# Sixteen heads: the first block's maxima between the steps of the last chunk's chain, projections beside the mixture, one stage elsewhere in memory

## The chip, the cores and the metric

The kernel runs on one core of a Trainium2 chip, in one launch. The metric is the device time of one execution in microseconds (us); the median of three runs is compared. A core has a matrix engine, TensorE (PE; its weight loads are listed apart, as PEld), three engines for everything else, VectorE (DVE), ScalarE (ACT) and GpSimd (POOL), and SyncE (SP), which here issues nearly all transfers (DMAs). Each engine works through its own list of instructions in the order that was fixed when the program was built, and waits where an instruction needs a result of another engine. Data lie in an on-chip memory of 128 partitions (SBUF); matrix products land in eight accumulation banks (PSUM), from which the other engines read them.

## The reference, cut to what matters

A residual stream `x` of 2048 tokens and 128 channels, in float32, goes through twelve steps. Each normalises `x`, computes something and adds it back, the feed-forward parts by half:

```python
x = x + 0.5 * L0_ffn(ln(x)); x = x + L0_attn(ln(x)); x = x + 0.5 * L0_ffn(ln(x))
x = x + 0.5 * L1_ffn(ln(x)); x = x + L1_attn(ln(x)); x = x + 0.5 * L1_ffn(ln(x))
x = x + 0.5 * L2_ffn(ln(x)); x = x + L2_attn(ln(x)); x = x + 0.5 * L2_ffn(ln(x))
x = x + 0.5 * L3_ffn(ln(x)); x = x + L3_attn(ln(x)); x = x + 0.5 * L3_ffn(ln(x))
```

Three of these functions matter here:

```python
def L1_attn(x):                       # 16 heads of 8 channels, every token sees every token
    q, k, v = heads(x @ w_qkv.T)
    attn = softmax((q * 8 ** -0.5) @ k.T)
    return merge(attn @ v) @ w_proj.T + b_proj
def L2_attn(x):                       # the same, q and k rotated by position, no bias
    q, k, v = heads(x @ Wqkv)
    q, k = q * cos + rotate_half(q) * sin, k * cos + rotate_half(k) * sin
    ...
def L1_ffn(x):                        # "the mixture": a shared expert and eight gated ones
    w = the two largest gates of softmax(ln'(x) @ gate_w.T), made to sum to one
    return swiglu_shared(x) + sum(w[:, e] * swiglu_e(x) for e in range(8))
def L2_ffn(x):                        # "the quantised stage"
    scale = max over blocks of 32 of |x| / 7.5; round x / scale to the FP6 grid; same for W
    return dequantised(x) @ dequantised(W).T + bias
```

## The kernel before, in words

**Tiles.** The 2048 tokens are four chunks (`NC` = 4) of `CH` = 512, a chunk is `TC` = 4 tiles of `P` = 128. `xs[c]` holds chunk c of the stream on chip through all twelve stages; nothing of it goes to memory between them. The stages in order are ffn0, attn0, ffn0, ffn1 (the first mixture), attn1 (the first attention of sixteen heads), ffn1 (the second mixture), ffn2 (the quantised stage), attn2 (the second attention of sixteen heads), ffn2, ffn3, attn3, ffn3; k counts a function's first and second use.

**Stages as generators.** Each stage is a Python generator that issues instructions and gives control back at its `yield`s. Class `Stage` (L2066 to 2111) holds one. `prepare` opens the stage's early memory pool on one of two sides of the memory, left or right in turn (`sides[n % 2]`), lets `pre_...` fetch weights, and makes the generator. While a stage runs it can call `io.lead(passed)`: this lowers the next stage's `due` by the time said to have passed, and when that is at or under 0 advances the next stage by one step. `mark(c)` tells that chunk c of a stage is done, `ready(c)` asks that of the stage before, `here()` asks whether the stage is the running one; `upcoming()` prepares the next stage. `yield True` says that what can be led is done; then the main loop (L2121 to 2128) runs the generator to its end when its turn comes. So the last chunk's work of each stage, which needs the previous stage's last chunk, stands at the seam of two stages. A scheduler settles each engine's list from the order of issue, with two exceptions: instructions kept in program order (`pe(...)`), and a context of high priority, whose instructions are put ahead.

**The mixture** (ffn1, L664 to 760). For each chunk nine experts follow each other. `up` makes twelve products of 512 columns, a SiLU on ACT and the product `h` on DVE (L717); `down` makes the products `pd` (L725, sixteen matmuls in the trace) and adds each tile into `xs[c]`, weighted by the gate, on DVE (L735). In the second mixture, with the quantised stage's steps between, 26 of these `h` start from 1574.6 to 1698.0 us, one every 4.9. After each expert of chunks 2 and 3 stands `if c > 1: io.lead(4.3)` (L756).

**The quantised stage** (ffn2, L807 to 838, with `quantised`, L763 to 794). Per chunk: statistics, `rs` (power on POOL, L143), `xn`, ten DVE operations of quantising (scales, `y`, `e2`, `big`) with one on POOL, four transposes, a copy `qT` on ACT, four products, an addition into `xs[c]`. In its first use chunks 0 to 2 are led beside the second mixture and the fourth stands behind it; its tiles have two buffers there.

**The sixteen-head attentions** (`packed`, L1296 to 1622, which attn0 with eight heads also uses). Per chunk, `front` transposes the normalised chunk and splits it into a high and a low part (`xH`, `xL`); `queries_or_keys(n, c)` multiplies by weights split in the same way (three products of 512 columns for `product`; attn2 makes two such products, multiplies each by a table and adds them on POOL: `rotated`, L1680, six products) and splits the result again (`kH`, `kL`, `qH`, `qL`). `stack_k` and `stack_q` copy rows of these by DMA (`rows_of`, three DMAs each, on SP's queue) into tiles `km` and `qt`, where a head's eight channels stand beside their low parts and constant rows; POOL fills the tiles by memsets first (L1493 to 1496). Before, the part that can be led (L1343 to 1354) makes the fronts and keys of chunks 0 to 2 and the queries of chunk 0, but the tiles, memsets and copies come behind `yield True`, so when the stage runs.

**Two passes of softmax** (`flash`, L970 to 1264). The work is cut into blocks n = (head group of 4 heads, query chunk): 16 blocks for each attention. `stream_a` is the first pass: for each block 32 steps, each with two score products (L1069, 512 columns each, into a pair of banks `s1`, of which there are two) and a maximum over 2 x 512 scores on DVE (L1087, at high priority). A step's keys come from one chunk; in block 0 the order is chunk pairs outside, query tiles, then the two chunks of the pair. When the 32 are through, DVE forms `mx` (L1095), and `put_max` folds it into the queries (`q2`). `stream_b` is the second pass: scores again (L1190), now with the maximum subtracted in the product, exp on ACT (L1199), products with the values (`pv`, L1136). It is a block or so behind the first pass, so within an attention both run side by side; at its start only the first pass can run. `hook` puts work at points of the first pass: the last chunk's front and keys (`ensure(NC - 1)`) at block 0's start, values, and the next queries (`queue`). Edges that the program adds (`last_of`, `last_top`) hold the first maximum of a group of steps behind a given DVE instruction.

Of the kernel before, what the change touches and what calls it, by code (L numbers as in the profile page):

```python
# [9 lines left out]
F32 = mybir.dt.float32  # L10
# [54 lines left out]
def tile_macaron(ctx: ExitStack, tc: tile.TileContext, a: dict, out: bass.AP, stages=STAGES):  # L65
# [598 lines left out]
    def ffn1(io, k, w, early):  # L664
# [35 lines left out]
        with tc.tile_pool(name="f1", bufs=1) as pool, tc.tile_pool(name="f1w", bufs=1) as pool_w:  # L700
# [42 lines left out]
            for c in range(NC):  # L743
                xT, gate = cur
                for n, e in enumerate(order):
# [10 lines left out]
                    if c > 1:  # L756
                        io.lead(4.3)
# [5 lines left out]
    def quantised(src, pool, tag, bufs=1):  # L763
# [5 lines left out]
        def new(name, m=n):  # L769
            return pool.tile([P, m], F32, name=name, tag=tag + name, bufs=bufs)  # L770
# [25 lines left out]
    def pre_ffn2(k, pool):  # L796
        if k == 0:
            w = fetch(pool, "l2w", 0, C)
            wqT.append(const.tile([P, P], F32, name="wqT"))
            q = quantised(w, pool, "w")  # L800
# [6 lines left out]
    def ffn2(io, k, w, early):  # L807
        bufs = 2 if k == 0 else 1
        half_bias = early.tile([P, C], F32, name="half_bias")
        nc.vector.tensor_scalar_mul(half_bias, row("bias2"), 0.5)  # L810
        for c in range(NC):
            while not io.ready(c):
                yield 0
            if c == NC - 1:
                yield True
                io.upcoming()
                io.lead(9.0)
            xn = layer_norm(c, True)
            q = quantised(xn.rearrange("p i c -> p (i c)"), early, "x", bufs)
            if io.here():  # L820
                for _ in range(8):
# [3 lines left out]
            qT = early.tile([P, CH], F32, name="qT", tag="qT", bufs=bufs)  # L825
# [9 lines left out]
            io.mark(c)  # L835
            if c < NC - 1:
                yield 1.0
                stats_of[c] = statistics_of(xs[c])

# [130 lines left out]
    def flash(io, pool, early, its, nh, causal, scale, s1, s2, pv_mm, put_max, begin, finish, poll=None,  # L970
              on_exp=None, split_at=1, fill=None, leads=None, hook=None, flush=True, order=None):
# [30 lines left out]
        if halved:  # L1002

            halves = {}
            for name in ("ident", "maskq", "maskk"):
                raw = pool.tile([P, 2, P], F32, name="halfraw", tag="halfraw", bufs=2)
# [5 lines left out]
                halves[name] = pool.tile([P, 2, P], BF16, name="half" + name)  # L1012
# [11 lines left out]
        if tiled and causal:  # L1024
            junk = pool.tile([P, CH], F32, name="junk")
            strip = pool.tile([P, CH], F32, name="strip")
# [4 lines left out]
        last_top = {}  # L1031
# [16 lines left out]

        def stream_a():
            for n, (g, qc) in enumerate(its):  # L1050
                begin(n)
                nk = chunks(qc)
                npair = (nk + 1) // 2
                mp = pool.tile([P, TC, nh, NC], F32, name="mp", tag="mp", bufs=3)
                for pi in range(npair):
                    for r in range(TC):
                        before = hook(n, pi, r) if hook is not None else None
                        if pi == r == 0 and before is None:
                            before = last_top.get(n - 1)
                        for kc in range(2 * pi, min(2 * pi + 2, nk)):  # L1060
                            for j0 in range(0, nh, 2):
                                ps = first_pass_bank()
# [1231 lines left out]
```

## Time and profile before

| What | us |
|---|---|
| Median of three runs (3746.23, 3755.47, 3755.72) | 3755.47 |
| The profiled execution, whole | 3769.46 |
| Its span, first to last instruction | 3767.7 |
| PE busy, 25325 matmuls | 3420.8 (91%) |
| DVE busy, 4793 instructions | 2870.9 (76%) |
| ACT busy, 3838 instructions | 2036.2 (54%) |
| POOL busy, 830 instructions | 828.8 (22%) |
| Mean granted clock of PE, as a share of full speed | 0.943 |

The stretches around the change, from windows of the trace (busy time of each engine, granted clock of PE):

| Stretch | From, to | Length | PE | DVE | ACT | POOL | Clock |
|---|---|---|---|---|---|---|---|
| First mixture's end to attn1's first `mx` | 817.5, 874.0 | 56.5 | 30.7 | 44.9 | 5.8 | 7.5 | 0.54 |
| attn1 from there, most of it | 874.0, 1340.0 | 466.1 | 449.7 | 443.7 | 399.7 | 0.0 | 0.99 |
| Second mixture, chunks 1 to 3 | 1580.0, 1702.7 | 122.7 | 120.5 | 88.9 | 37.4 | 13.6 | 1.00 |
| Second mixture's end to attn2's first `mx` | 1702.7, 1780.6 | 77.9 | 47.1 | 66.1 | 12.6 | 18.5 | 0.59 |
| attn2 from there, most of it | 1780.6, 2300.0 | 519.4 | 499.6 | 494.8 | 443.1 | 2.6 | 0.99 |

The table is read by rows: an engine whose busy time is close to the length sets that stretch's pace. Times of single instructions count from the start of the profiled execution's span. The second mixture's row begins at a round number somewhat after that stage's start and shows the engines' loads there.

### The profile page before, as it was taken

How to read it: one execution, taken by the hardware profiler on the slowest of the kernel's cores; microseconds unless marked ns; L12 is line 12 of the kernel's file. 1: busy time of each engine (PE TensorE's matmuls, PEld its weight loads, DVE VectorE, ACT ScalarE, POOL GpSimd, SP SyncE). 2: the span in 40 equal slices, each digit the busy share in tenths (PEclk: the TensorE clock that was granted, in tenths of full speed). 3: DMA queues.
4: the chain of work that ended last, by engine and by line, in shares of the span. 5: the costliest groups of instructions: out<-in, count | busy, mean ns of one | idle time of the engine just before them, and what ended most of it. 6: DMA issues, size and time to landing. Idle time of an engine off the chain costs nothing. (4 is left out here: it accounts for less than half of the span.)

```text
span 3767.7 us, 64628 instructions
## 1 busy us (share of the span) xinstructions
PE 3420.8 (91%) x25325; PEld 1846.5 (49%) x25325; DVE 2870.9 (76%) x4793; ACT 2036.2 (54%) x3838; POOL 828.8 (22%) x830
## 2 busy tenths in 40 slices
PE   7679987978999999996999999888999999999989
PEld 5543356863333333783333333366444444444458
DVE  6488555768999998668899999654777877788862
ACT  3246732325888888421788888732333444444442
POOL 1511124110000000112000000142555445533341
PEclk9779988987999999996999999998899999999999
DMA  3311023000000000102000000012443232221010
GB/s 104 83 49 29 9 81 95 4 26 5 12 12 14 8 3 1 35 1 70 10 14 6 16 5 4 15 46 75 140 147 112 97 106 97 89 63 52 24 34 12
DMA packets 124689, 170.18 MB, mean 45 GB/s; under 512 B 25120, under 2 KB 52514, under 8 KB 124384
## 3 DMA queue, kind: packets, MB, share of 16 engines
q1 hardware_dynamic: 121824, 160.80, 13.7%
q0 software_dynamic: 2560, 5.25, 0.9%
q8 instruction: 199, 3.26, 0.3%
q14 instruction: 106, 0.87, 0.1%
HBM read 101.25 MB, written 45.87 MB: 39 GB/s over the span
## 5 line engine op out<-in xcount | busy, mean ns | idle before, releaser
L1087 DVE TENSOR_REDUCE mp<-s 128x2 f32<-128x1024 f32 (+3 forms) x1440 | 1625.7, 1181 | 88.5 <-PE s L1069 68.1
L1199 ACT ACTIVATE pt<-s 128x512 f32<-128x512 f32 (+1 forms) x2368 | 1220.7, 601 | 216.4 <-PE s L1190 141.8
L1190 PE MATMUL s<-q,km 32*128 32x512 f32 (+2 forms) x2368 | 733.6, 491 | 28.6 <-ACT pt L1199 18.7
L1136 PE MATMUL pv<-pt,v 128*32 128x256 f32 (+1 forms) x8568 | 730.9, 413 | 22.9 <-ACT ov L1577 11.2
L1069 PE MATMUL s<-km,qt 32*128 32x512 f32 (+3 forms) x2368 | 620.0, 507 | 61.1 <-DVE mp L1087 37.1
L1190 PEld LDWEIGHTS s<-q,km 32*128 32x128 f32 (+1 forms) x2368 | 324.1, 184 | 531.6 <-issue 341.3
L1179 ACT ACTIVATE pt<-s 128x512 f32<-128x512 f32 (+3 forms) x640 | 306.2, 530 | 355.7 <-PE s L1171 212.8
L143 POOL TENSOR_TENSOR rs<-rs,minus_half 128x4 f32<-128x4 f32 x56 | 57.5, 1026 | 1543.7 <-DVE rs L142 1542.7
L1993 DVE TENSOR_TENSOR sum<-sum,pt 128x512 f32<-128x512 f32 (+3 forms) x328 | 259.4, 805 | 89.9 <-ACT pt L1179 88.3
L1136 PEld LDWEIGHTS pv<-pt,v 128*32 128x32 f32 x8568 | 169.1, 108 | 316.4 <-issue 146.3
L1171 PE MATMUL s<-q,k 64*128 64x512 f32 (+3 forms) x1920 | 300.0, 403 | 14.7 <-ACT pt L1179 10.4
L1136 PE MATMUL pv<-pt,latv 128*64 128x512 f32 (+3 forms) x1280 | 310.4, 564 | 1.3 <-ACT pt L1179 1.3
L1993 POOL TENSOR_TENSOR sum<-sum,pt 128x512 f32<-128x512 f32 (+1 forms) x200 | 265.6, 1328 | 181.5 <-ACT pt L1179 177.0
L1069 PEld LDWEIGHTS s<-km,qt 32*128 32x128 f32 (+1 forms) x2368 | 236.4, 191 | 124.1 <-DVE mp L1087 82.3
L1171 PEld LDWEIGHTS s<-q,k 64*128 64x128 f32 x1920 | 161.8, 188 | 224.8 <-issue 137.3
L715 ACT ACTIVATE sg<-pg 128x1024 f32<-128x1024 f32 x72 | 73.9, 1027 | 174.4 <-PE pg L229 158.8
L1069 PE MATMUL s<-k,q 64*128 64x512 f32 (+3 forms) x640 | 133.7, 433 | 19.0 <-DVE mp L1087 18.6
L1791 DVE TENSOR_TENSOR rot<-rot,tab 128x512 f32<-128x512 f32 x128 | 87.7, 685 | 74.2 <-PE rot L229 38.4
L725 PEld LDWEIGHTS pd<-l1d,h 128*128 128x128 f32 x1152 | 139.3, 192 | 5.6
L725 PE MATMUL pd<-l1d,h 128*128 128x128 f32 x1152 | 140.1, 275 | 0.0
L717 DVE TENSOR_TENSOR h<-pu,sg 128x1024 f32<-128x1024 f32 x72 | 87.9, 1220 | 60.6 <-PE pu L229 55.7
L1171 PE MATMUL s<-q,two 64*128 64x512 f32 (+3 forms) x640 | 128.0, 368 | 0.0
(575 smaller groups left out, 4696.7 us busy)
## 6 DMA issues: line engine op xcount, KB each, us to landing
tab<-in_l3rope SPq DMA_DIRECT2D x66, 256.0 KB
q<-q SPq DMA_DIRECT2D x32, 512.0 KB
k<-k SPq DMA_DIRECT2D x32, 512.0 KB
l0e<-in_l0e SPq DMA_DIRECT2D x32, 256.0 KB
q<-h SPq DMA_DIRECT2D x32, 256.0 KB
q<-rot SPq DMA_DIRECT2D x32, 256.0 KB
k<-h SPq DMA_DIRECT2D x32, 256.0 KB
k<-rot SPq DMA_DIRECT2D x32, 256.0 KB
```

The costliest lines, as they stand in the source:

```text
L715: nc.scalar.activation(sg, pg, AF.Silu)
L717: nc.vector.tensor_tensor(h.rearrange("p m n -> p (m n)"), pu, sg, ALU.mult)
L725: nc.tensor.matmul(pd[:, i, :], h[:, m, i * P : (i + 1) * P], wd[:, m, :], start=m == 0, stop=m == 1,)
L1069: pe(nc.tensor.matmul(ps[:, o : o + w], lhsT, rhs[:, :w], start=True, stop=not masked))
L1087: ins = nc.vector.tensor_reduce(mp[:, r, j0 : j0 + 2, kc], both[:, :, :w], AX.X, ALU.max,)
L1136: i = pe(nc.tensor.matmul(pv[out_rows, lo:hi], lhsT, pts[j][:, lo:hi], start=kt == 0, stop=kt == nt - 1 and hi == CH))
L1171: pe(nc.tensor.matmul(outs[j][:, c0:], lhsT, rhs[:, c0:], start=i == 0, stop=i == len(terms[0]) - 1 and not diag,))
L1179: ex = nc.scalar.activation(pts[j][:, c0:], outs[j][:, c0:], AF.Exp, scale=scale)
L1190: pe(nc.tensor.matmul(ps[:, c0:], lhsT, rhs[:, c0:], start=i == 0, stop=i == len(terms) - 1 and (tiled or not diag),))
L1199: ex = nc.scalar.activation(pt[:, c0:], ps[:, c0:], AF.Exp, scale=scale)
L1791: nc.vector.tensor_tensor(t.bitcast(F32), ps, halves["tabs"][i], ALU.mult)
L1993: eng.tensor_tensor(t[:, c0:], other[:, c0:], pts[j][:, c0:], ALU.add)
```

## The change

Both programs compute the same thing with the same instructions on PE, DVE, ACT and POOL; SP issues two DMAs more. What changes is where they are issued.

1. `flash` becomes a generator with a number of steps `ahead`. With it, block 0's steps go chunk by chunk of the keys (all four query tiles on chunk 0's keys, then on chunk 1's, and so on), and the first 24 of its 32 steps, which need the keys of chunks 0 to 2 alone, are given out one at a time, each behind a `yield`, and without high priority.
2. In `packed` the helpers move ahead of the part that is led. That part now also fills and stacks the keys of chunks 0 to 2 and the queries of chunk 0, makes chunk 1's queries, and then gives out the 24 steps with an infinite `due` until the last chunk's `ensure(NC - 1)`, at high priority, when the stage runs. Three of the eight `km` tiles and one of the three `qt` tiles lie in the stage's early pool.
3. The second mixture leads from its second chunk on (`c > 1 or c and k`). `lead` advances the next two stages, and preparing the quantised stage prepares attn2 with it, so attn2's projections of chunks 0 to 2 and both queries are led during the second mixture.
4. The quantised stage's last chunk runs at high priority, after all of attn2's led part has been issued (`lead_all`). Its tiles have one buffer, and tags shared with the weights' quantising; `qT` takes the place of `big`; its statistics come ahead of `mark`.
5. attn2 lies on the same side of the memory as the quantised stage (`side_of`, `between`), whose second use shares the pool of the first. `pre_attn1` and `pre_attn2` fetch the projections' weights into a scratch tile, and the others by a DMA of their own. attn2 keeps its output tiles `ov` and `oT` in the pool `att`.

```diff
@@ ffn1
-                    if c > 1:
+                    if c > 1 or c and k:
                         io.lead(4.3)
@@ quantised
-    def quantised(src, pool, tag, bufs=1):
+    def quantised(src, pool, tag):
...
-            return pool.tile([P, m], F32, name=name, tag=tag + name, bufs=bufs)
+            full = CH if m == n else CH // 32
+            return pool.tile([P, full], F32, name=name, tag=tag + name, bufs=1)[:, :m]
@@ ffn2
-                io.lead(9.0)
+                if k == 0:
+                    io.lead_all()
+            urgent.enter_context(tc.high_priority() if c == NC - 1 and k == 0 else nullcontext())
             xn = layer_norm(c, True)
-            q = quantised(xn.rearrange("p i c -> p (i c)"), early, "x", bufs)
-            if io.here():
-                for _ in range(8):
+            q = quantised(xn.rearrange("p i c -> p (i c)"), early, "x")
+            if io.here() and k:
+                for _ in range(9):
                     io.lead(9.0)
...
-            qT = early.tile([P, CH], F32, name="qT", tag="qT", bufs=bufs)
+            qT = early.tile([P, CH], F32, name="qT", tag="xbig", bufs=1)
@@ flash
+        def some(n, turns, mp):
+            g, qc = its[n]
...
+            for first, (r, kcs) in enumerate(turns):
+                before = hook(n, kcs[0], r) if hook is not None else None
...
+                for kc in kcs:
+                    for j0 in range(0, nh, 2):
+                        ps = first_pass_bank()
...
+                        with tc.high_priority() if not waiting[0] else nullcontext():
...
+                                ins = nc.vector.tensor_reduce(
+                                    mp[:, r, j0 : j0 + 2, kc], both[:, :, :w], AX.X, ALU.max,
+                                )
...
+                        yield 2 * w if tiled else w
...
         def stream_a():
+            if ahead:
+                mp = early.tile([P, TC, nh, NC], F32, name="mp0")
+                begin(0)
+                yield from some(0, [(r, [kc]) for kc in range(NC) for r in range(TC)], mp)
+                maxima(0, mp)
...
+        if ahead:
+            waiting[0] = True
+            for _ in range(ahead):
+                step_a()
+                yield
+            waiting[0] = False
@@ packed
+            ahead=0 if causal else 2 * TC * (NC - 1),
+        )
+        if not causal:
+            new_k(early)
+            new_q(early)
         for c in range(1 if causal else NC - 1):
...
+            stack_k(0, c)
+            keyed[0] = c + 1
+            if c == 0:
+                stack_q(*its[0])
+            if c < 2:
+                new_k(early)
+            yield 1.5
+            if c == 1:
+                queries_or_keys(0, 1)
+                yield 1.5
+        if not causal:
+            for _ in range(2 * TC * (NC - 1)):
+                yield 1e9
+                next(flow)
         yield True
...
-            if not causal:
-                ensure(NC - 2)
+            else:
+                with tc.high_priority():
+                    ensure(NC - 1)
...
+            for _ in flow:
+                pass
@@ pre_attn2
-        w = fetch(pool, "l2a", 0, 6 * C)
-        parts = [split(w[:, n * C : (n + 1) * C], pool, f"w{n}") for n in range(4)]
+        raw = scratch(F32, "raw")
+        nc.sync.dma_start(out=raw, in_=a["l2a"][:, : 4 * C])
+        parts = [split(raw[:, n * C : (n + 1) * C], pool, f"w{n}") for n in range(4)]
+        w = fetch(pool, "l2a", 4 * C, 6 * C)
@@ Stage
+            if name == "ffn2" and k == 0:
+                shared.append(pool)
+                line[self.n + 1].prepare()
...
+        def lead_all(self):
+            s = line[self.n + 1]
+            while not s.led:
+                s.step()
...
-            if self.n + 1 < len(line):
-                s = line[self.n + 1]
+            for s in line[self.n + 1 : self.n + 3]:
                 s.due -= passed
                 if s.steps is not None and not s.led and s.due <= 0.0:
                     s.step()
+    shared = []
+    between = [n for n in range(1, len(stages)) if stages[n - 1] == ("ffn2", 0)]
+
+    def side_of(n):
+        return sides[n % 2 if n not in between else (n - 1) % 2]
```

## The prediction

> **What bounds the kernel now.** I read the slices of the page first, then windows of 5 us where a slice showed a slow TensorE clock, then the order of time there.
>
> ```profile
> PE   7679987978999999996999999888999999999989
> DVE  6488555768999998668899999654777877788862
> PEclk9779988987999999996999999998899999999999
> ```
>
> One slice is 94.2 us. Slices 9 to 15 and 19 to 24 are the two attentions of sixteen heads: PE and DVE both at 9, so nothing is gained inside them. Slices 8 and 18 are how they begin: PE at 7 and 6, clock 0.7 and 0.6. Windows there:
>
> ```profile
> 810.00:815.00 5.00, 5.00 (x37) 4.63 (x36) 2.83 (x8) 1.03 (x1) 0.00 (x0) 1.00 0.01 3
> 830.00:835.00 5.00, 0.03 (x1) 0.00 (x0) 1.23 (x4) 0.92 (x2) 0.00 (x0) 0.76 0.28 70
> 855.00:860.00 5.00, 3.48 (x10) 1.14 (x8) 5.00 (x5) 0.00 (x0) 0.00 (x0) 0.50 0.00 0
> 900.00:905.00 5.00, 4.54 (x47) 1.47 (x47) 3.98 (x4) 3.41 (x8) 0.00 (x0) 1.00 0.01 3
> 1725.00:1730.00 5.00, 4.32 (x12) 3.20 (x13) 2.73 (x4) 1.69 (x3) 1.75 (x2) 0.50 0.41 123
> 1760.00:1765.00 5.00, 3.38 (x10) 1.15 (x8) 5.00 (x6) 0.00 (x0) 0.00 (x0) 0.50 0.00 0
> ```
>
> Columns: length, busy PE, weight load, DVE, ACT, POOL, granted clock, DMA. First PE alone is full (the mixture). Then nothing is (830, 1725: the chain that makes the last chunk's keys). Then DVE alone is full and ACT idle (855, 1760: the first block's maxima, before which no exp can start). In order of time (start, length, engine, line):
>
> ```profile
> 817.15 0.32 DVE L735 SCALAR_TENSOR_TENSOR x<-pd,gate,x 128x128 f32<-128x128 f32 x1
> 823.16 8.45 SPq L1379 DMA_DIRECT2D qt<-qH  x4
> 836.57 0.80 PE L1069 MATMUL s<-km,qt 32*128 32x512 f32 x4 [6.54 <-issue]
> 837.40 36.29 DVE L1087 TENSOR_REDUCE mp<-s 128x2 f32<-128x1024 f32 x32 [5.97 <-PE s L1069]
> 873.73 0.22 DVE L1095 TENSOR_REDUCE mx<-mp 128x16 f32<-128x64 f32 x1
> ...
> 1701.53 1.13 DVE L735 SCALAR_TENSOR_TENSOR x<-pd,gate,x 128x128 f32<-128x128 f32 x4 [0.66 <-PE pd L725]
> 1741.12 4.65 DVE L1087 TENSOR_REDUCE mp<-s 128x2 f32<-128x1024 f32 x4
> 1780.38 0.21 DVE L1095 TENSOR_REDUCE mx<-mp 128x16 f32<-128x64 f32 x1
> ```
>
> From the mixture's last addition into x to `mx`: 873.73 - 817.47 = 56.3 us in the first attention, 1780.38 - 1702.66 = 77.7 us in the second. Of both, 32 x 1.134 = 36.3 are maxima; the rest, 20.0 and 41.4, is chain, where DVE mostly waits. What follows `mx` (five more maxima, the folding of the maximum, the first exp 8.0 us later) has the same order in both builds.
>
> **The change, part by part.** On PE, DVE, ACT and POOL both built programs have the same number of instructions; two DMAs are added. So it is order alone, and I price the order.
>
> *First maxima between the chain's steps, first attention.* 24 of the 32 need chunks 0 to 2 only, whose keys are ready beside the mixture. In the built order they stand on DVE one by one between the chain's steps, which are then: statistics and rs 1.0, xn 1.1 (row `xn` x4 1.11 at 1735), xL 0.69, kL 0.69, copies 0.35, together 3.8. PE is in order too, with transposes and products put among the scores, so DVE still waits: 0.4 for the first score; 0.6 for the power, which now stands behind seven memsets on POOL (7 x 0.48 from 817.7, then 1.03, ready at 822.1, when three maxima are through at 821.5); 0.7 where transposes and copy (1.12 + 0.59 and hand-offs) outlast one maximum. Sum 36.3 + 3.8 + 1.7 = 41.8 against 56.3: **-14.5**. This removes the wait of the queue row too: the first query's low part stood on SP behind copies that waited 8.45 us for chunk 1's queries. Its three copies and the nine of keys 0 to 2 are now issued beside the mixture, past no weight that is fetched later there. The last keys' copies are three issues of 0.59 and 2.4 from the last issue to the score that waited for it (834.20 to 836.57): due at about 833 and needed at about 851, so covered by the maxima still to come.
> *Its cost:* chunk 1's queries move into the first mixture, where PE is full: 3 products x 0.228 (start to start there) = **+0.7**. Four memsets (1.9 of POOL) move with them, POOL being nearly idle.
>
> *The same, second attention.* Two chains follow each other: the quantised stage's last chunk, then this attention's. DVE steps between maxima: statistics 0.9, mr 0.16, quantising 0.69 + 0.18 + 0.25 + 0.69 + 0.41 + 0.41 + 0.68 + 0.68 + 0.69, x 0.69, statistics 1.4, xn 1.11, xL 0.69, two rotations 1.38, kL 0.68, copy 0.21, together 11.9. Waits that a maximum or two (1.13 each) doesn't fill: transposes, copy, product (1.05 + 0.59 + 2.08) 1.7; transposes and copy 0.8; six products at 0.42 0.7; first score 0.4; the last keys' landing 0.9: 4.5. Sum 36.3 + 11.9 + 4.5 = 52.7 against 77.7: **-25.0**.
>
> *Its cost, all other projections beside the second mixture.* Before, keys of chunks 0 to 2 and the queries of chunk 0 ran between 1701 and 1740, chunk 1's queries among the maxima. Now 5 x 6 = 30 products x 0.228 = 6.8 and 12 transposes x 0.122 (16 in 1.95) = 1.5 stand in PE's queue there: +8.3, in full, for:
>
> ```profile
> 1580.00:1623.00 43.00, 42.76 (x270) 37.98 (x269) 30.60 (x84) 12.63 (x13) 2.30 (x2) 1.00 0.00 1
> 1623.00:1660.00 37.00, 36.28 (x237) 32.41 (x237) 27.34 (x83) 13.28 (x17) 4.60 (x4) 1.00 0.00 1
> 1660.00:1702.00 42.00, 41.48 (x266) 36.58 (x264) 30.30 (x86) 10.81 (x14) 6.07 (x6) 1.00 0.00 1
> ```
>
> PE is busy 120.5 of 122. DVE's 88.2 gets some 16 more (10 rotations, 3 xL, 5 low parts at 0.69, xn 3 x 1.1), 104 of 130: not the bound on average, but in bursts. Where keys' and queries' rotations of chunk 0 stand together, DVE has about 9 us of work between two `h` that come every 4.5; PE can run ahead about 3. I take 2.7 for the bursts. Bounds: 0 (DVE's mean is under PE's) to 20 (each of the five projections holds `h` by the 4.4 that rotation, addition, copy and low part took from 1713.34 to 1717.8). Nearest is the low end, since this mixture already carries the quantised stage's chunks with 1.5 idle. So **+11.0**. Waiting behind on SP: the queries' tables, which reuse the keys' tiles; of the mixture's weights none is fetched behind that wait.
>
> *Weights split out of a scratch tile, one buffer instead of two in the quantised stage, the pool shared by its two runs, the second attention's place in memory:* nothing added. They are hidden by the mixture (the attention's weights, fetched at 1702.86 before, now come during the mixture), or three steps of one chunk follow each other anyway; if the cover went, a chunk's quantising would wait for the transposes of the one before, at most the 1.0 that these take, three times. Its second run orders the next stage's first transposes a little later: 0, bounds -1.5 to +1.5 (one transposition and copy, 1.06 + 0.59).
>
> A rule speaks against the POOL work that this puts beside the mixture. The row first: `y` took 1.48 at 1578.84, beside POOL's addition of 1.27, and 0.68 at 1583.93 without one.
>
> ```profile
> 1578.50 1.27 POOL L827 TENSOR_TENSOR x<-x,half_bias 128x512 f32<-128x512 f32 x1
> 1578.84 1.48 DVE L780 TENSOR_TENSOR y<-xn,inv 128x512 f32<-128x512 f32 x1
> 1583.93 0.68 DVE L791 TENSOR_TENSOR y<-y,big 128x512 f32<-128x512 f32 x1
> ```
>
> The Trainium skill, page "SBUF — State Buffer", section "Who interferes with whom", has it that a VectorE instruction with two SBUF inputs and a GpSimd one that reads SBUF exclude each other, the later one waiting for the whole of the other; the trace agrees within its 0.8. By it the five added rotations' additions could each hold DVE by up to 1.3, 6 us, and if PE paid all of it the sum would be about -22.
>
> **Sum:** -14.5 + 0.7 - 25.0 + 11.0 = **-27.8**. Against the profiled execution (span 3767.7, whole 3769.5) that is 3739.9 and 3741.7. The runs shown have a median of 3755.5, 14 below the profiled one; I take the difference over to it: **3728**.
>
> **Rivals.**
> *A, more is won.* The bursts cost nothing and the clock, 0.50 while PE was 70% busy in 855 to 860, stays at 1.0 because scores follow the mixture without a hole: six products at 0.23 instead of 0.42 win 1.1, and the fold of the maximum and the first scores (0.80 + 0.65 + 0.80 at the half clock) as much again, each time. -27.8 - 2.7 - 4.4 = -35: 3720. Against: DVE, not PE, paces the maxima, so PE will have holes.
> *B, the chain runs no faster than its waits.* PE is in order: a transpose that waits holds the scores behind it, DVE starves, and chain and maxima come one after the other. At most the chain's waits outside DVE come back: in the second power 4.6, xn 1.7, POOL 1.3, product 3.7 and keys 6, in the first keys 3: about 20, so -8 and 3748. For it: the order is fixed when built. Against: between two chain steps stand one or two maxima, about as long as each wait.
> *C, slower: the second mixture breaks up.* The place: chunks 1 to 3. Fourteen groups (three transposes and five projections of the attention, three transposes and three products of the quantised stage, now closer together) wait in PE's queue for DVE, POOL and ACT. If each is late by one chain of 4.4, that is 62 + 8.3 + 0.7 - 39.5 = +31: 3787. It breaks even at 2.2 a group. Against: PE idles 1.5 of 122 there with six of the groups in it.
> *D, the change doesn't do it:* the maxima are held until the chain is through, by a wait that the order doesn't show (a score bank, a memset of reused memory). Then the first attention wins only SP's wait, 836.6 - 833.2 = 3.4, and pays 0.7. In the second, chain and maxima follow each other: 11.9 + 17 (B's waits there) + 4.2 for the copies + 36.3 = 69 against 77.7, less the 11.0: +2. Together -0.4: 3755.
>
> **How the numbers follow.** Chances: forecast (-18 to -34) 0.60, A 0.10, B 0.13, C 0.10, D 0.07. What a measurement here can tell from no change is 0.3%, 11 us. Faster: forecast, A and 0.05 of B: 0.75. Same: the rest of B, D and 0.01 of C: 0.16. Slower by over 0.3%: 0.09. The range takes in A's end with the runs' own spread of 9 (3712) and B (3750); C is left out.
>
> **What would show it.** After the first mixture, maxima from within 1 us of its end, `mx` some 42 us after its last addition (56.3 now); after the second some 53 (77.7 now), DVE near 5.0 of 5 in all windows between; the second mixture's chunks 1 to 3 about 11 us longer with PE still near full; the attentions' inner windows as now. Wrong if PE idles over 10 us more in that mixture (C), or if DVE has holes of several us between maxima (B, D).

## The result, and the profile after

The changed kernel took 3734.48 us (median of 11 runs, 3729.47 to 3745.57), the kernel before, run beside it, 3752.33 us (11 runs, 3744.12 to 3763.63): a ratio of 0.9956, with a 95% interval of 0.9941 to 0.997. On another occasion, with 7 and 12 runs, the ratio was 0.9958 (0.9944 to 0.9973). So the change wins about 16 us. The forecast was 27.8 us won and 3728. The time lies in its range, 6.5 above the point; the win lies below the 18 to 34 that the forecast gave its likeliest case.

The two profiled spans, 3767.7 and 3729.6, differ by 38.1, and that is not the change alone: 13.2 of it lie ahead of the first mixture's second chunk, where both programs do the same in nearly the same order (in a second profile of the changed kernel that part is as long as in the kernel before, 689.3 against 688.2 us). The kernel before had medians from 3752 to 3770 us on the five occasions on which it was run, so times of different occasions are not compared here; ratios are. Lengths of the same stretch, between the same instructions, repeat far better: where an edit left them alone, within 0.5 us, but for chunk 0 of the second mixture and the last row of the table below, which vary by up to 2. The account is made by them. Of the kernel before there is one profile, so its lengths stand without a repeat.

First the slices of the page of the changed kernel (a slice is 93.2 us now, 94.2 before, so the digits shift a little along the row):

```profile
PE   8679988989999999997999999898999999999999
DVE  6578556778999996778999999654767877788852
PEclk9779998988999999996999999898899999999999
```

Counted from 0, slices 8 and 18, where the two sixteen-head attentions begin, are at 8 and 7 of 10 for PE instead of 7 and 6. The places can still be seen: the clock falls to 0.8 and 0.6 there.

Next the stretches of the changed kernel around the change, by windows (start and end, length, then busy time of PE, weight loads, DVE, ACT and POOL, granted clock, DMA). The first is from the first mixture's last addition into x to `mx`, the second the second mixture's chunk 0, the third its chunks 1 to 3, the fourth from its last addition to `mx`:

```profile
804.04:845.82 41.78, 28.33 (x79) 12.21 (x79) 39.75 (x47) 5.26 (x11) 5.58 (x9) 0.54 0.11 28
1497.63:1544.72 47.09, 43.52 (x264) 37.57 (x265) 33.82 (x79) 13.38 (x15) 14.78 (x17) 1.00 0.33 100
1544.72:1690.85 146.13, 140.19 (x874) 122.53 (x872) 117.10 (x340) 47.82 (x64) 25.76 (x25) 1.00 0.08 24
1690.85:1742.27 51.42, 30.46 (x94) 14.60 (x94) 47.09 (x70) 5.81 (x14) 7.52 (x9) 0.57 0.12 33
```

And the same stretches of the kernel before:

```profile
817.47:873.95 56.48, 30.74 (x86) 13.46 (x86) 44.86 (x47) 5.75 (x12) 7.49 (x13) 0.54 0.14 35
1525.07:1570.09 45.02, 43.37 (x264) 37.65 (x265) 31.75 (x80) 13.40 (x15) 10.72 (x9) 1.00 0.26 72
1570.09:1702.66 132.57, 130.43 (x831) 115.92 (x830) 97.76 (x284) 41.09 (x52) 16.89 (x17) 1.00 0.00 1
1702.66:1780.59 77.93, 47.12 (x136) 24.45 (x136) 66.06 (x103) 12.59 (x26) 18.46 (x23) 0.59 0.28 84
```

Lengths tell it: 56.48 has become 41.78, 77.93 has become 51.42, and 45.02 + 132.57 = 177.59 has become 47.09 + 146.13 = 193.22. In the two stretches to `mx` DVE was busy 79% and 85% of the time and is now 95% and 92%.

The order of the first attention's beginning in the changed kernel (start, length, engine, line), on DVE:

```profile
803.72 0.32 DVE L735 SCALAR_TENSOR_TENSOR x<-pd,gate,x 128x128 f32<-128x128 f32 x1
804.43 1.20 DVE L1089 TENSOR_REDUCE mp<-s 128x2 f32<-128x1024 f32 x1
...
808.59 1.12 DVE L166 TENSOR_SCALAR xn<-x,mv,rs 128x128 f32<-128x128 f32 x4 [0.57 <-POOL rs L143]
809.62 1.22 DVE L1089 TENSOR_REDUCE mp<-s 128x2 f32<-128x1024 f32 x1
...
815.09 0.69 DVE L1360 TENSOR_TENSOR kL<-pq,kH 128x512 fp32r<-128x512 f32 x1 [0.96 <-ACT kH L1359]
816.05 29.51 DVE L1089 TENSOR_REDUCE mp<-s 128x2 f32<-128x1024 f32 x26 [0.27 <-PE s L1071]
...
845.60 0.22 DVE L1100 TENSOR_REDUCE mx<-mp 128x16 f32<-128x64 f32 x1
```

The first maximum runs 0.4 us after the last addition. Chain steps (`xn`, `kL`) stand between maxima. DVE's waits left in the stretch add up to 2.0 us; three of them are shown, in square brackets with the instruction that ended them.

| Stretch (us) | Before | After | Difference | Forecast |
|---|---|---|---|---|
| First mixture, last addition of chunk 0 to that of chunk 3 | 129.3 | 129.0 | -0.2 | +0.7 |
| To `mx`, first attention | 56.5 | 41.8 | -14.7 | -14.5 |
| Second mixture, first `h` to last addition | 177.6 | 193.2 | +15.6 | +11.0 |
| To `mx`, second attention | 77.9 | 51.4 | -26.5 | -25.0 |
| Second attention's last addition to the next but one stage's first | 55.0 | 59.1 | +4.1 | 0 |

The last row runs across the quantised stage's second use to the first addition of the stage behind it (ffn3, called the ternary stage below). In eight other profiles with the change's order there it is 59.0 to 61.2, so the loss is 4 to 6 us. The five rows make -21.7, and with 61 in the last one -20; the interval of the ratio stands for 11 to 22 us.

### The profile page after: what moved, and what is told of

Its sections match the earlier page's. It is cut to its first block, busy times and chain, and to the rows that moved or that the text cites. A ratio compares the mean times of both kernels' runs of the same rounds, so it can differ in the third digit from the quotient of the medians.

```text
span 3729.6 us, 64652 instructions
## 1 busy us (share of the span) xinstructions
PE 3409.1 (91%) x25325; PEld 1839.7 (49%) x25325; DVE 2862.6 (77%) x4793; ACT 2035.6 (55%) x3838; POOL 826.4 (22%) x830
## 5 line engine op out<-in xcount | busy, mean ns | idle before, releaser
L717 DVE TENSOR_TENSOR h<-pu,sg 128x1024 f32<-128x1024 f32 x72 | 87.8, 1220 | 51.3 <-PE pu L229 46.1
```

Source lines behind the costliest of these rows:

```text
L717: nc.vector.tensor_tensor(h.rearrange("p m n -> p (m n)"), pu, sg, ALU.mult)
```

## The experiments

All are edits of the changed kernel. For each, what was expected is quoted as it was put on record; "the change" means the changed kernel.

### What the order is worth: maxima behind the chain again

```diff
-            for _ in range(2 * TC * (NC - 1)):
-                yield 1e9
-                next(flow)
...
+            if n == kc == r == 0:
+                return last_of[1, NC - 1]
```

> The 24 first maxima of both attentions are issued behind the last chunk's keys, and the first of them is held behind kL, as before the change; keys 0 to 2 and the first query are still stacked, and projected, beside the mixtures. Theory (the win is the order on DVE, chain and maxima filling each other's waits): from the mixture's last addition to mx the first attention takes 20.0 - 3.4 + 36.3 = 53 us (41.8 with the change, 56.5 before), the second 11.9 + 17 + 4.2 + 36.3 = 69 (51.4 with the change, 77.9 before); the mixtures stay as with the change. In all 29 us more than the change, some 3763, that is slower than the kernel before. Rival (the win is that copies, memsets and projections have left the seam): both stretches stay near 42 and 51, the time near 3734.

Ratio to the kernel before 0.9998 (0.9982 to 1.0014): no gain is left, but no loss either. The stretches to `mx` were 46.2 and 62.9, between both theories. (The second mixture took 194.5; 1.5 of that is a stretch of lower clock, which comes up again below.) On DVE, first attention:

```profile
821.69 1.66 DVE L166 TENSOR_SCALAR xn<-x,mv,rs 128x128 f32<-128x128 f32 x4 [1.20 <-POOL rs L143]
...
828.29 0.69 DVE L1360 TENSOR_TENSOR kL<-pq,kH 128x512 fp32r<-128x512 f32 x1 [2.91 <-ACT kH L1359]
828.90 36.28 DVE L1089 TENSOR_REDUCE mp<-s 128x2 f32<-128x1024 f32 x32
```

and the same step in the kernel before, with POOL's memsets beside it:

```profile
819.80 2.86 POOL L1494 MEMSET km<- 128x512 f32 x6
819.89 4.83 DVE L166 TENSOR_SCALAR xn<-x,mv,rs 128x128 f32<-128x128 f32 x4 [1.21 <-POOL rs L143]
822.60 1.47 POOL L1496 MEMSET qt<- 128x512 f32 x3
```

So the first attention's 14.7 us have two parts. The order, chain steps between maxima, is worth 46.2 - 41.8 = 4.4. The other 10.3 come from work that has left the chain: `xn` ended with POOL's memsets at 824 and took 4.83 where 1.66 do without so many of them, and the first maximum came at 837.4, behind copies on SP's queue that waited for chunk 1's queries, where in this run it follows `kL` at once (9.6 us after the last addition instead of 19.9). In the second attention the order is worth 62.9 - 51.4 = 11.5 of 26.5; there the chain is two stages long, with more waits to fill. These are the prices of the order once the rest has left the chain; no run puts maxima between the steps of the long chain with memsets and copies still in it.

### What the projections cost, beside the mixture or behind it

```diff
-            for s in line[self.n + 1 : self.n + 3]:
+            for s in line[self.n + 1 : self.n + 2]:
```

> The second mixture leads the quantised stage alone; the second attention's fronts and projections of chunks 0 to 2 are issued at its end, ahead of the interleaved maxima. Theory (beside the mixture they cost PE's 8.3 us and some 5 of waits, at the seam DVE's time): the mixture goes from 193.2 us (first h of chunk 0 to the last addition) back to about 180, the stretch to mx from 51.4 to some 68 (DVE gets 10 rotations, 3 xL, 5 low parts at 0.69, 3.3 of xn = 15.7), net 3 more than the change, near 3738. Rival (moving the projections was a loss, since at the seam they fit into the chain's waits): mixture 180, stretch 57 to 60, net 5 to 7 less than the change, 3728.

Ratio 0.9973 (0.9958 to 0.9988). The mixture took 182.4, the stretch to `mx` 70.5: 10.8 less and 19.1 more than with the change, so by these stretches moving the projections wins 8.3 us (the two ratios stand for about 6, and their intervals overlap). The theory had the side right, and its price at the seam was 2.5 too small. Over the whole second mixture, with the change and then in this run:

```profile
1497.63:1690.85 193.22, 183.71 (x1135) 160.10 (x1135) 150.92 (x419) 61.21 (x79) 40.53 (x42) 1.00 0.14 43
```

```profile
1511.19:1693.62 182.43, 174.90 (x1094) 153.39 (x1094) 137.26 (x401) 55.24 (x68) 34.19 (x37) 1.00 0.09 26
```

PE's busy time differs by 8.8 of the 10.8: products are paid in full, and DVE's 13.7 us of added work cost little. But 182.4 is still 4.8 more than the 177.6 of the kernel before, with PE busy 1.1 more: waits that are not the projections'.

The 8.3 hold against projections that stand ahead of the maxima. In this run's stretch to `mx`,

```profile
1693.62:1764.12 70.50, 47.38 (x136) 23.37 (x135) 59.14 (x88) 11.84 (x24) 13.97 (x14) 0.60 0.25 73
```

DVE waits 11.4 us, against 4.3 with the change, and its busy time is 12.0 more. If maxima were put between the projections too and covered those waits, the seam would lose some 12 (an estimate from these two busy times), little more than the 10.8 that the mixture pays. No run does that.

### Is PE the payer? One product in place of three

```diff
-                scratch, parts[2 * n], parts[2 * n + 1], lambda ps, w: product(ps, w, xT),
+                scratch, parts[2 * n], parts[2 * n + 1],
+                lambda ps, w: nc.tensor.matmul(ps, w[0], xT[0], start=True, stop=True),
```

> Each projection of the second attention's queries and keys makes one product (high by high) instead of three; the two products with low parts are left out, so 20 products of 512 columns fewer stand in the second mixture. Theory (there PE pays for every product put in, 0.228 us each): the mixture goes from 193.2 to 188.6. Rival (DVE's bursts set the length): it stays at 193 +- 1. The stretch to mx loses at most 4 x 0.42 = 1.7 of its 51.4.

The mixture took 188.74, that is 4.5 less for 20 products: 0.224 each. PE pays, DVE's bursts don't set the length. The stretch to `mx` was 50.1.

### The mixture's other 4.8 us

Leading the quantised stage from chunk 2 on, with the projections out of the mixture:

```diff
-                    if c > 1 or c and k:
+                    if c > 1:
...
-            for s in line[self.n + 1 : self.n + 3]:
+            for s in line[self.n + 1 : self.n + 2]:
```

> As the run that leads the quantised stage alone beside the second mixture, and the leading begins with chunk 2, as before the change. That run's mixture is 182.4 us, 4.8 more than before the change, with no more work on PE. Theory (2.1 of it are chunk 0's late h, the rest comes from quantised chunks that are led one chunk earlier and meet the mixture's own routing on DVE): 180 here. Rival (single buffers and shared tiles cause the rest): stays at 182.4.

181.6, on the face of it neither theory. Chunks 1 to 3 took 133.1, near the 132.6 of the kernel before (135.3 in the run that leads the quantised stage alone), so the earlier start of leading costs 2.2 us there. Chunk 0, which the edit doesn't touch, took 48.5 instead of 47.1. That is the clock. The same 4 us of chunk 0, in this run and then with the change:

```profile
1529.60:1533.60 4.00, 3.99 (x15) 3.49 (x16) 3.28 (x9) 0.00 (x0) 1.99 (x3) 0.57 0.07 23
1518.00:1522.00 4.00, 3.95 (x28) 3.67 (x29) 3.43 (x10) 0.01 (x1) 1.95 (x3) 1.00 0.09 32
```

PE gets through 15 matmuls instead of 28 at a granted clock of 0.57, and the time from the fifth `h` to the sixth is 7.1 instead of 5.6. The run with the maxima behind the chain has the same 7.1, at 0.57 too; the twelve other profiles have 1.00 over chunk 0. Without these 1.5 us the mixture is 180.1, which is the theory's 180. So of the 4.8 us, 2.1 are chunk 0's (47.1 less 45.0), 2.2 the earlier leading, and 0.5 are left.

Then the transposes of the quantised chunk, later by one expert (`yield 9.0` becomes `yield 13.0`):

> The quantised stage's transposes come one expert later in the mixture's queue (its step is due after 13 instead of 9). In the second mixture PE waits 1.26 + 1.26 + 0.50 us for the quantised chunk, out of 7.9 idle. Theory (PE waits since DVE's quantising is queued close to the transposes): 3 us of the 193.2 go, to 190, the rest unchanged. Rival (DVE's work comes in bursts and whoever is next waits): the wait moves to the products or to h, and the mixture stays at 193 +- 1.

The mixture took 194.3, so the theory falls; the rival's 193 +- 1 was passed by 0.3. PE's waits for the transposes, such as this one of the change,

```profile
1562.37 0.66 PE L180 MATMUL turn<-cst,e 128*128 128x128 f32 x4 [1.26 <-DVE e L794]
```

went, and in their place PE waited 1.69 and 1.89 us for `h`, which stood behind the same DVE work. In that mixture it is a matter of who waits for DVE's quantising, not of whether.

Two trials at chunk 0. In the first the second attention was prepared during chunk 1:

```diff
-                line[self.n + 1].prepare()
...
+                    if k and c == 1 and n == 1:
+                        line[io.n + 2].prepare()
```

> The second attention's weights are fetched and split, and its tiles filled, during the second mixture's chunk 1 instead of chunk 0. Theory (in chunk 0 these casts and POOL's splits and memsets stand beside the mixture's own weight splits and make one h late by 2.1 us): first h of chunk 0 to first h of chunk 1 goes from 47.1 to 45.2, the whole mixture from 193.2 to 191.3. Rival (the same work hinders chunk 1 as much): the whole stays at 193.

Chunk 0 stayed at 47.1, the mixture at 193.25. But the trace shows the casts `w0H` and `w1H` at the same place as with the change, 13.2 us behind the first `h`: the scheduler had brought them forward again, and the weights' transfers too, so this run does not decide. In the next pair of runs they were tied to an instruction, the last `h` of chunk 0, and as a second edit, told of in the next part, nine and four steps of the ternary stage were led ahead of the quantised stage's last normalising:

```diff
+            split(raw[:, n * C : (n + 1) * C], pool, f"w{n}", after=newest_h[0])
...
+                    for _ in range(9):
+                        io.lead(9.0)
...
-                for _ in range(9):
+                for _ in range(0):
                     io.lead(9.0)
```

With four steps the two ranges are 4 and 5.

> Two edits, far apart in time. First: the four casts of the second attention's weights (and with them POOL's four subtractions) are held behind the newest h issued, the last of the second mixture's chunk 0. Theory (in chunk 0 they stand among the mixture's own splits and with POOL's make an h 2 us late): first h of chunk 0 to first h of chunk 1 goes from 47.1 to 45.3, the mixture from 193.2 to 191.4. Rival (the memsets ahead of wgu0L, or the quantised weights, cause it): stays at 47. Second: in the quantised stage's second use all nine steps of the next stage are led ahead of the last chunk's normalising (one before the change, none with it). Theory (that chunk is needed last, and its 8 us of DVE and 3.5 of POOL stand in the way of the next stage's first products): from the attention's last addition to the next stage's first addition 50 to 54 us, against 59 to 61 with the change and 55 before. Rival (the next stage's start waits for its weights and PE alone): stays near 57, what leading one step gave.

> The same hold on the casts, and four of the nine steps led ahead of the last chunk's normalising. By the theory of the run beside it: the mixture again 191.4, and the stretch from the attention's last addition to the next stage's first addition between that run's and 57. By the rivals: 193.2 and 57.

Chunk 0 took 46.3 and 46.1, the mixture 192.5 and 192.2: half of what was expected at most, since without the hold and at full clock chunk 0 ranges from 46.6 to 47.2 over eight profiles. Some 0.7 us of chunk 0's 2.1 are the casts. The place where PE idles longest, with the change:

```profile
1514.84 1.33 POOL L222 TENSOR_TENSOR wgu5L<-l1w,wgu5H 128x512 fp32r<-128x512 f32 x1 [0.36 <-DVE wgu5H L218]
1514.95 1.30 DVE L790 TENSOR_SCALAR big<-e 128x128 f32<-128x128 f32 x1
...
1516.79 1.21 DVE L717 TENSOR_TENSOR h<-pu,sg 128x1024 f32<-128x1024 f32 x1
```

`big`, a step of quantising the quantised stage's weights, ends with POOL's subtraction and takes 1.30, and `h`, for which PE idles 2.1, stands behind it. But this is not the casts' price. The subtraction splits weights of the mixture's own expert 5; with the casts held it still holds `big`, and in the kernel before, where `big` took 0.23, it held `e`, the step ahead of it, which takes 0.21 with the change. With the casts held, then before:

```profile
1527.82 0.92 DVE L218 CAST wgu5H<-l1w 128x512 fp32r<-128x512 f32 x1 [0.71 <-DMA l1w<-in_l1w]
...
1528.90 1.28 DVE L794 TENSOR_SCALAR big<-e 128x128 f32<-128x128 f32 x1
```

```profile
1539.51 0.61 DVE L218 CAST wgu5H<-l1w 128x512 fp32r<-128x512 f32 x1
...
1540.35 1.19 DVE L785 TENSOR_SCALAR e<-y 128x128 int32<-128x128 int32 x1
```

What does differ is the cast ahead of it: 14.4 us behind the first `h` and without a wait before, 15.2 to 16.7 us behind it in all profiles with the change's order, where in twelve of thirteen it waits 0.15 to 1.45 for the expert's weights. Six transfers for the second attention (its weights and four tables) now stand between the mixture's weights on SP's queue there. That they make these weights late fits the rows but was not tested; no run moved them. So some 1.3 us of chunk 0 (46.3 less 45.0) stay open.

### The quantised stage's second use

```diff
+                else:
+                    io.lead(9.0)
             urgent.enter_context(tc.high_priority() if c == NC - 1 and k == 0 else nullcontext())
...
-                for _ in range(9):
+                for _ in range(8):
```

> In the quantised stage's second use the next stage's first step is led ahead of the last chunk's normalising again, as before, and eight after its quantising. With the change the stretch from the attention's last addition to the first addition of the ternary stage is 59.1 us, before it was 55.1. Theory (the order alone: three xn of 1.3 us stand beside POOL's weight splits, and the next stage's first transposes come 5 us later): back to 55 +- 1. Rival (the single buffer and the tile that qT shares make the chunk wait): stays at 59.

57.2 against 59.0 to 61.2 with the change: the order explains 2 to 4 of its 4 to 6 us. The rows of the change beside the ones of POOL show what stands in the way with the change's order:

```profile
2407.43 5.79 DVE L166 TENSOR_SCALAR xn<-x,mv,rs 128x128 f32<-128x128 f32 x11
2408.62 1.30 POOL L222 TENSOR_TENSOR w0L<-l3w,w0H 128x512 fp32r<-128x512 f32 x1 [1.31 <-ACT w0H L218]
2409.89 1.26 POOL L222 TENSOR_TENSOR w1L<-l3w,w1H 128x512 fp32r<-128x512 f32 x1
2411.11 1.26 POOL L830 TENSOR_TENSOR x<-x,half_bias 128x512 f32<-128x512 f32 x1
```

Three of the `xn`, 0.34 alone, end with POOL's three instructions and take 1.3. In the kernel before, `w0L` and `w1L` ran ahead of this. With the order put back they still don't: `w0L` holds `mr`, a step of the last chunk's normalising (1.23, alone 0.16), and two `xn` stand beside `w1L` and the addition:

```profile
2421.01 1.23 DVE L157 SCALAR_TENSOR_TENSOR mr<-mv,rs 128x4 f32<-128x4 f32 x1 [1.12 <-POOL rs L143]
2422.16 4.09 DVE L166 TENSOR_SCALAR xn<-x,mv,rs 128x128 f32<-128x128 f32 x8
```

```profile
2420.94 1.28 POOL L222 TENSOR_TENSOR w0L<-l3w,w0H 128x512 fp32r<-128x512 f32 x1
2423.35 1.30 POOL L222 TENSOR_TENSOR w1L<-l3w,w1H 128x512 fp32r<-128x512 f32 x1 [1.13 <-ACT w1H L218]
```

So the 2 us that are left may be these, or the single buffer that the rival names; no run parts them. The two runs above, with four and nine steps led first, have 59.1 and 67.5. So more of it is worse, and the theory that the last chunk only stands in the way falls.

### Going further, and a version of its own

Maxima given out within the mixtures, while the next chunk is awaited:

```diff
-                    if c > 1 or c and k:
+                    if c:
                         io.lead(4.3)
...
+                if c and not causal and given[0] < 2 * TC * c:
+                    given[0] += 1
+                    next(flow)
                 yield 0
```

> A further step: while an attention's led part waits for the next chunk of its input, it gives out first maxima for keys that are ready, one for each expert, nine in the first mixture (which now also leads from its second chunk on) and eight in the second. Each puts two score products (0.46 us) into PE's queue in the mixture and takes 1.13 us of DVE from the seam. Theory: the first mixture (last addition of chunk 0 to the last of chunk 3) goes from 129.0 to 133.2, the stretch to mx from 41.8 to 31.6; the second mixture from 193.2 to 196.9, its stretch from 51.4 to 42.3; net 11.5 less than the change. Rival (scores take the pair of banks that the experts' products need, and each step makes the mixture wait 2 us): the mixtures get 34 us longer, net 15 more than the change.

Ratio 1.0007 (0.9995 to 1.0019), the gain is gone. The first stretch to `mx` is 31.6, as worked out, the second 48.8. But the mixtures took 144.2 and 209.7, which is 15.2 and 16.4 more for nine steps each (the trace has nine in the second as well), 1.7 and 1.8 a step; the first mixture's leading also starts a chunk earlier here, which is in its 15.2. On PE, in the second mixture of this run:

```profile
1625.73 0.50 PE L1071 MATMUL s<-km,qt 32*128 32x512 f32 x2
1627.84 0.50 PE L227 MATMUL pg<-xTH,wgu2H 128*128 128x512 f32 x1 [1.62 <-DVE h L717]
```

The scores take one of the two pairs of banks, and the next expert's product waits for the pair that `h` still reads: the rival's mechanism, and nearly its price. Three such waits make 4.4 us. The other parts of the 16.4 are the products themselves, 18 x 0.228 = 4.1, and slow clock behind the longest holes, as here, behind waits of 2.55 and 0.91 us:

```profile
1645.00:1650.00 5.00, 5.00 (x17) 3.95 (x17) 3.97 (x15) 0.23 (x1) 0.00 (x0) 0.50 0.00 0
```

Over the five windows of 5 us where the clock is under 1.00 (0.91, 0.50, 0.91, 0.84, 0.82) that loses some 5 us, an estimate from these clocks. The seam is the cheap place for maxima.

Last, the change and a version with three edits side by side: casts held, one step led first, and the attentions' last chunk normalised on ACT.

> The changed kernel itself, on the same chip as the run beside it. Theory: every stretch as in its first profile (mixtures 129.0 and 193.2, to mx 41.8 and 51.4), and 16 to 20 us under the kernel before, so a ratio near 0.995. Rival (the first profile's 38 us between both spans were the change's): a ratio near 0.990.

> Three edits on the changed kernel: the weights' casts held behind chunk 0 of the second mixture, one step of the next stage led ahead of the quantised stage's last normalising in its second use, and both sixteen-head attentions' last chunk normalised on ACT (four of 0.49) instead of DVE (1.12). Theory: second mixture 192.3 (193.2), the attention's last addition to the next stage's first 57.2 (59 to 61), each stretch to mx 0.9 less (40.9 and 50.5): 5 us under the changed kernel, a ratio to the kernel before near 0.994. Rival (with DVE's step gone, the longer chain is no longer covered by the 24 maxima, and the last keys' landing shows): the stretches to mx stay or grow by up to 1.5, and the whole is within 2 us of the changed kernel.

The change repeated itself: 0.9958, stretches 129.0, 41.8, 192.8, 51.6. The version had 0.9951 (0.9938 to 0.9963); the intervals overlap, so it is not shown to be faster. Its mixture (192.3) and the stretch across the quantised stage (57.6) did what was expected, and ACT did not: 43.2 and 54.3 to `mx`, 1.5 and 2.7 longer. In the second attention DVE waits 2.59 for the last keys, with one maximum left behind `kL` to cover their copies instead of three:

```profile
1742.82 1.22 DVE L1096 TENSOR_REDUCE mp<-s 128x2 f32<-128x1024 f32 x1
1747.03 9.14 DVE L1096 TENSOR_REDUCE mp<-s 128x2 f32<-128x1024 f32 x8 [2.59 <-PE s L1078]
```

The chain had become the longer of the two, and what it gained on DVE was not the bound.

## Why the prediction was right, and where it was off

**The sum.** The two gains were met, and the cost of the projections; two terms that the sum put at nothing cost 4.8 and 4 to 6. So the rows make -20 to -21.7 instead of -27.8, and the runs some -16. That the time came within 6.5 of 3728 is partly luck: the kernel before had 3752.3 over eleven runs where the sum was taken off 3755.5. Of the readings that it began with, one is a slice off (the clock of 0.7 is slice 9's, slice 8 has 0.8), and DVE stands at 8, not 9, in slices 9, 15 and 19; no term hangs on either.

**The two chains.** Right in size, -14.7 and -26.5 for -14.5 and -25.0, and in what would be seen: maxima from 0.4 us behind the mixture's end, `mx` 41.6 us after the last addition (42 forecast) and 51.2 (53). The sum of DVE's own instructions and a few short waits is what the stretch takes. But the reason was told too simply. In the first attention only 4.4 us come from the order; 10.3 come from memsets, copies and chunk 1's queries that left the chain, and of the second's 26.5 only 11.5 come from the order. The working noted that the queue's wait ends and left the memsets at the cost of a later power; that they also held `xn` for over 3 us could be read in the row of 4.83 and was not.

**The cost of the projections.** +11.0 forecast, 10.8 measured by taking them out. Of its parts PE's 8.3 were 8.8, and the 2.7 for bursts were 2.0.

**"Nothing added", the weights, the single buffer, the place in memory.** This step failed: 4.8 us of waits in the second mixture, 2.1 in chunk 0, of which the split of the attention's weights explains some 0.7, and 2.7 behind it, of which leading one chunk earlier explains 2.2. Behind chunk 0 the single buffer is left with 0.5 at most; in the trace the quantised chunks' last steps are 50 and 45 us apart (1573.6, 1623.5 and 1668.3), and a chunk takes some 20 from its first `xn` to its last step. The Trainium skill's page "SBUF — State Buffer", section "Who interferes with whom", was quoted for added POOL work and set aside with "about -22" for the sum. The rows' -20 to -21.7 come near that by luck: of the five rotations' additions one held DVE, at an `mr`, 1.22 for 0.15, where the working had 1.3 for each.

**"0, bounds -1.5 to +1.5" for the quantised stage's second use.** Failed as well: +4 to +6, of which the order of one step against the last chunk's normalising explains 2 to 4; the rest is open. The step was priced as a transposition and a copy; what it moved was three `xn` beside POOL's weight splits and its addition.

**The rivals.** A, the clock stays at 1.0: no, it is 0.54 and 0.57 in the stretches. B, the chain's waits return: no, DVE idles 2.0 and 4.3 there. C, the mixture breaks up: no, though its bounds were where the loss came from; chunks 1 to 3 are 13.6 longer (11 forecast), and PE idles 9.5 us in the whole mixture (193.2 less 183.7) instead of 3.8, which is 0.4 for each of fourteen groups, far from 2.2. D did not happen, but the run that makes it happen shows its price wrong: 46.2 and 62.9, not 53 and 69, since the chain without copies and memsets is 9.9 and 26.6 long. The total of D, no change, was met (0.9998), by luck: the two stretches are 13 us shorter than it had them, and the mixture and the quantised stage's second use took about as much.

## What to carry to other kernels

Where an engine in order works off a long chain with waits, independent work of the same engine given out one instruction at a time between its steps costs its own length and no more; look for such work where a reduction must pass over everything before the next engine can begin. Work taken off that chain may be worth more than the order: memsets, copies and a projection that are done beside an earlier stage paid 10 us here. Moving work beside a stage whose engine is full costs that engine's time in full, and the small items that come with it (an earlier start, weight casts, perhaps transfers) cost nearly half as much again; price them by the rows of the engine that both share, and try an edit that makes the cover do more before believing in it: a pair of scores in the mixture cost 1.7 to 1.8 us for 1.1 won. And before a stretch of a single profile is held against a theory, look at its granted clock: here 1.5 us of slow clock hid that a theory was right.

## What the runs showed of the hardware that was not expected

POOL's memsets, which read nothing, held DVE's `xn`: 4.83 us for four where 1.11 do without them, and the last `xn` ends within 0.7 us of the last memset. It was not one memset that was waited out but a run of nine, of about 0.48 each. The maxima were not held by POOL: 1.20 to 1.23 us each beside memsets and beside subtractions, 1.16 to 1.23 with POOL idle. The Trainium skill's page "SBUF — State Buffer", section "Who interferes with whom", has both, that a `tensor_scalar` or a cast may take the pair of ports shared with GpSimd and then one waits for the whole of the other, and that `tensor_reduce` never does; these rows agree.

A hole of PE in the second mixture's chunk 0, of 1.8 and 2.2 us, was followed in two profiles by 4 us at a clock of 0.57; in the eleven others with the change's order, holes of 1.2 to 2.2 us at the same place were not. What decides it the runs don't show.
